# Second products of the first two expert tiles in front of the first products of tiles 2 and 3, in a fused two-layer Flamingo block

## The chip, the cores and the metric

The kernel runs on one NeuronCore of one Trainium2 chip. The metric is the device time of one execution in microseconds. Each kernel is run several times and the median counts; beside it stands one execution taken by the hardware profiler, from which all profile lines come.

## The reference

Inputs are x (4 x 512 x 512, float32) and the weights of four sublayers, each added to x behind a gate. The first three (an int8-quantised product pair, a ternary feed-forward, and cross attention with 16 heads) are not touched here. The last is a mixture of 8 experts, of which each token takes two:

```python
router_in = norm_w * (xf * rsqrt(mean(xf * xf) + EPS))
probs = softmax(router_in @ router_w.T)
topw, topi = top_k(probs, 2);  topw = topw / sum(topw)
cw = zeros((T, E)).at[arange(T)[:, None], topi].add(topw)
g = einsum('td,edf->tef', flat, gate_w);  u = einsum('td,edf->tef', flat, up_w)
expert_out = einsum('tef,efd->ted', silu(g) * u, down_w)
y = einsum('ted,te->td', expert_out, cw) * 4
x = x + tanh(g_ffn[1]) * y
```

T is 2048 tokens, D is 512, and the hidden width of an expert is 256.

## The kernel before

The four batches (512 tokens each) are worked through layer by layer. Everything up to the attention of the last batch is the same before and after. What matters begins near 1300 us of the profile.

**Routing and sorting.** `route(b)` computes the router of one batch: it first stores the batch's `x` after attention to `out` (L771), normalises the rows (`xnl` for the last batch, L184), turns them with PE (L790) into `xTl` (copies by ACT L126 and DVE L128), multiplies with the router's weights (L807), turns the logits (L819) and ranks the experts. Normalised rows and gate weights go to a table in DRAM, `xtab`. `sort` groups the (token, expert) pairs by expert into tiles of 128 rows. Part "a" sorts the first three batches into 16 full tiles (0 to 15) before the last batch's attention is through; part "b" sorts the rest, when the last batch has been routed. In all 36 tiles are sure to be worked.

**One tile.** `gather` (L1076) fetches the 128 rows of the tile out of `xtab` by an indirect DMA that GpSimd (POOL) issues. `weigh_rows` (L1085, L1086, DVE) finds each row's gate weight in them. The rows are turned, by PE for some tiles (`by_tensor`: 0 to 7, 16 to 19 and the last; `prepare`, L1188 with an ACT copy) and by DVE and 16 DMAs on SP's queue for the others (`turn_rows`, L577 and L1179, four tiles at a time). `expert_in` reads the expert's number into a register of PE (L1090), does the first product (L1093, four matmuls of two passes each), Silu on ACT (L1094) and the product of gate and up with the row weight on DVE (L1095), which gives `hid`. `turn_hidden` turns `hid` with PE (L1188) and DVE copies it (L1189). `expert_out` does the second product (L1215), ACT copies it to `y` (L1219), and POOL issues an indirect DMA that adds `y` to the rows of `out` (L1220). Each such addition is made to wait for the one before it, and the first also for the stores of batches 0 to 2.

**Tiles 0 and 1.** Their first products stand between the last heads of the attention (`start_tile`, L1107 and L1093); `hid0` and `hid1` lie in their own buffers.

**The main loop.** For `j` from 0 on: gathers that are due (four tiles ahead for a tile turned by PE, ten ahead for the others), turns by DVE that are due, `hide` (first product of tile j; at j = 0 those of tiles 0 to 3, of which 0 and 1 are done already), `prepare` of tile j + 1, `turn_hidden` of tile j - 1, `expert_out` of tile j - 2, and two steps of the generators `beside`, which are the routing of the last batch and then the sort of part "b". So tile 0's second product comes at j = 2, tile 1's at j = 3.

**The order on the engines.** A scheduler orders the instructions of all engines from the program by its own priorities; each engine then works its queue in that order, and waits on semaphores where a buffer or a value is not ready. The program's order decides who is the earlier and who the later writer of `out`.

Of the kernel before, what the change touches and what calls it, by code (L numbers as in the profile page):

```python
# [57 lines left out]
def kernel(  # L58
# [82 lines left out]
    def acc_tile():  # L141
        sums_in[0] += 1
        return bank(4 + sums_in[0] % 4)
# [875 lines left out]
    def step_beside():  # L1019
        if beside:  # L1020
            try:
                next(beside[0])
            except StopIteration:
                beside.pop(0)
# [63 lines left out]
    def expert_in(j, xgT, h):  # L1088

        e = nc.tensor.value_load(found[j][1], min_val=0, max_val=NE - 1)  # L1090
        ps = work_tile() if j < len(first_hid) else acc_tile()
        for k in range(KD):
            nc.tensor.matmul(ps, lhsT=xgT[k], rhs=gu[:, bass.ds(e, 1), k, :], start=(k == 0), stop=(k == KD - 1))  # L1093
        nc.scalar.activation(h, ps[:, :FE], AF.Silu)  # L1094
        nc.vector.scalar_tensor_tensor(h, h, row_weight[:, j : j + 1], ps[:, FE:], ALU.mult, ALU.mult)  # L1095
        return e, h
# [3 lines left out]
    hidden, first = {}, {}  # L1100
# [57 lines left out]
    def fetch(j):  # L1158
        got[j] = gather(j, mo.tile([P, ROW], F32, tag="xg", name="xg", bufs=8))

    def turn_rows(j):


        if j in by_tensor:
            return
        g, t = divmod(j, NT)
        if t == 0:
            blocks_of[g] = mo.tile([P, NQ, KD * P], F32, tag="blocks", name="blocks", bufs=2)
        xg, owned = got.pop(j)
        tc.keep_in_program_order(  # L1170
            turn_tile_apart(xg[:, :D], blocks_of[g].rearrange("p c (s t r) -> p c s t r", s=KD, t=NT), t)
        )
        weigh_rows(j, xg, owned)
        if t == NT - 1:
            blocks = blocks_of.pop(g)
            dst = mo.tile([P, NQ * KD * P], F32, tag="turned", name="turned", bufs=2)
            for c in range(NQ):
                for a in range(NQ):
                    nc.sync.dma_start(  # L1179
                        dst[c * Q : (c + 1) * Q, a * KD * P : (a + 1) * KD * P], blocks[a * Q : (a + 1) * Q, c]  # L1180
                    )
            for u in range(NT):
                turned_in[g * NT + u] = [dst[:, k * NT + u :: KD * NT] for k in range(KD)]

    def turn_by_tensor(src, n, dst, copy=nc.vector.tensor_copy):
        tp = work_tile()
        for k in range(n):
            nc.tensor.transpose(tp[:, k * P : (k + 1) * P], src[:, k * P : (k + 1) * P], ident)  # L1188
        copy(dst, tp[:, : n * P])  # L1189
        return [dst[:, k * P : (k + 1) * P] for k in range(n)]  # L1190

    def prepare(j):
        if j in by_tensor and j not in hidden and j not in turned_in:
            dst = mo.tile([P, KD * P], F32, tag="xgT", name="xgT", bufs=2)
            turned_in[j] = turn_by_tensor(got[j][0], KD, dst, nc.scalar.copy)
            weigh_rows(j, *got.pop(j))

    def hide(j):
        if j not in hidden:
            prepare(j)  # L1200
            h = mo.tile([P, FE], F32, tag="hid", name="hid", bufs=3)
            hidden[j] = expert_in(j, turned_in.pop(j), h)

    def turn_hidden(j):
        e, h = hidden.pop(j)
        hT = turn_by_tensor(h, NF, mo.tile([P, NF * P], F32, tag="hidT", name="hidT", bufs=3))
        waiting[j] = (e, hT)
# [3 lines left out]
    def expert_out(j):  # L1211
        e, hT = waiting.pop(j)
        ps = acc_tile()
        for f in range(NF):
            nc.tensor.matmul(  # L1215
                ps, lhsT=hT[f], rhs=dn[:, bass.ds(e, 1), f, :], start=(f == 0), stop=(f == NF - 1)
            )
        y = mo.tile([P, D], F32, tag="y", name="y", bufs=3)
        nc.scalar.copy(y, ps)  # L1219
        add = nc.gpsimd.indirect_dma_start(  # L1220
            yacc,
            bass.IndirectOffsetOnAxis(ap=found[j][0], axis=0),
            y,
            None,
            bounds_check=TOK - 1,
            oob_is_err=False,
            compute_op=ALU.add,
        )
        if j in (0, NA):
            written.extend(stores[-1:] if j else stores[: B - 1])  # L1230
        for w in written:
            tc.add_manual_dep(
                add.ins,
                w.ins.name,
                mybir.DependencyInfo(mybir.DependencyClass.Sync, mybir.DependencyReason.DATA),
                reason="adds to what is there",
            )
        written[:] = [add]
# [10 lines left out]
    for j in range(NSURE + 1):  # L1249
        known = NSEG if len(found) == NSEG else NA  # L1250
        for t in [t for t in to_fetch if t - lead[t] <= j and t < known]:
            fetch(t)
            to_fetch.remove(t)
        while to_turn and to_turn[0] - TURN <= j and to_turn[0] in got:
            turn_rows(to_turn.pop(0))


        if j < NSURE - 1:
            for i in range(NT) if j == 0 else (j,):
                hide(i)  # L1260
        if j and j + 1 < NSURE:
            prepare(j + 1)
        if j:
            turn_hidden(j - 1)
        for i in (j - 2,) if j < NSURE - 1 else (j - 2, j - 1) if j == NSURE - 1 else (j - 1,):
            if i >= 0:
                expert_out(i)
        if j == NSURE - 1:
            hide(j)
        step_beside()  # L1270
        step_beside()
        if j == NA - 4:
            while beside:
                step_beside()

    n = nc.values_load(in_all[0:1, :], min_val=1, max_val=NSEG)  # L1276
    with tc.If(n > NSURE):
        for j in range(NSURE, NSEG):
            fetch(j)
        for j in range(NSURE, NSEG):  # L1280
            hide(j)
            turn_hidden(j)
            expert_out(j)
# [35 lines left out]
```

## Time and profile before

| | us |
|---|---|
| median of 3 runs | 1570.09 (1568.76 to 1570.95) |
| the profiled execution | 1567.48 |
| its span (first to last instruction) | 1565.7 |
| tile 0's first product (L1093) | from 1310.43 |
| first product of tiles 2 and 3 | from 1341.85 |
| router's product of the last batch (L807) | from 1355.88 |
| first addition to `out` (L1220) | 1356.77 |
| first product of tile 4 | from 1362.27 |
| last addition | 1557.47 |

The times in the rows are microseconds from the span's start. In a timeline row stand the start, the length, the engine (PE matmul, PEld weight load, DVE, ACT, POOL, SP; a "q" is its queue), the line, the operation, what it writes and reads, the count, and in brackets how long the engine had been idle and what ended that. In a row of stages stand the stage, its length, the busy time of PE, PEld, DVE, ACT and POOL with their counts, the clock granted to PE, the DMA engines' share and GB/s.

### The profile page before, as it was taken

Reading aid. Unit: us, or ns where it says so; the run is one execution under the profiler, and the core shown is the slowest. Engines: PE = TensorE matmul, PEld = TensorE weight load, DVE = VectorE, ACT = ScalarE, POOL = GpSimd, SP = SyncE. Lnnn points to the kernel's source line nnn. Section 1 sums busy time; section 2 is a strip of 40 time slices with the busy share of each in tenths; the row PEclk is TensorE's granted clock in tenths of the full one; section 3 lists DMA queues with packets and bytes.
Section 4 is the critical chain, followed back from the end, with each engine's and each line's share of the span. In section 5 each row is a group of like instructions: output and inputs, shape, how many; then the busy total and the mean of one; then the engine's idle time right before and its main releaser. Section 6 shows DMA issues by size and latency. Waiting matters only on the chain. (4 is left out here: it accounts for less than half of the span.)

```text
span 1565.7 us, 15898 instructions
## 1 busy us (share of the span) xinstructions
PE 1475.8 (94%) x4294; PEld 740.9 (47%) x4294; DVE 905.0 (58%) x2339; ACT 554.0 (35%) x1141; POOL 414.0 (26%) x540
## 2 busy tenths in 40 slices
PE   4988998899999999999999999999999998899995
PEld 2454656666544444444444444444444443455553
DVE  5898737556275555586565675665668553653320
ACT  3554453444243333253323353333433331412111
POOL 2232314352311113131131141141141111335422
PEclk9999999999999999999999999999999999999998
DMA  8633111013355445475455485475584653567542
GB/s 300 222 116 129 47 41 62 28 41 97 126 160 150 133 138 157 136 218 153 127 151 141 129 223 149 117 187 143 153 233 127 159 146 99 149 115 144 122 89 38
DMA packets 110840, 211.10 MB, mean 135 GB/s; under 512 B 28816, under 2 KB 32912, under 8 KB 110752
## 3 DMA queue, kind: packets, MB, share of 16 engines
q0 software_dynamic: 32736, 97.73, 24.0%
q1 hardware_dynamic: 70224, 100.74, 22.9%
q10 hardware_dynamic: 7792, 11.60, 2.1%
q8 instruction: 37, 0.61, 0.2%
q14 instruction: 51, 0.42, 0.1%
HBM read 95.34 MB, written 34.93 MB: 83 GB/s over the span
## 5 line engine op out<-in xcount | busy, mean ns | idle before, releaser
L674 DVE CUSTOM_DVE_ANT_0 e<-bank,mask_b 128x512 f32<-128x512 f32 x256 | 175.0, 688 | 245.7 <-PE bank L669 245.6
L694 PE MATMUL bank<-eT,v 128*128 128x512 f32 x512 | 230.5, 592 | 2.2 <-DVE nmax L674 2.2
L669 PE MATMUL bank<-kT,qT 128*128 128x512 f32 x512 | 231.1, 593 | 0.0
L708 PE MATMUL bank<-wo,oT 128*128 128x512 f32 x512 | 230.7, 592 | 0.3 <-ACT oT L698 0.3
L677 ACT ACTIVATE e<-e,nmax 128x512 f32<-128x512 f32 x256 | 184.3, 720 | 81.6 <-DVE nmax L674 74.5
L571 DVE STREAM_TRANSPOSE blocks<-e 128x512 f32<-128x512 f32 x256 | 158.9, 677 | 30.7 <-DMA eT<-blocks 26.1
L656 PE MATMUL bank<-gu,wq 128*128 128x512 f32 x384 | 174.9, 594 | 1.2 <-DVE nmax L674 1.2
L694 PEld LDWEIGHTS bank<-eT,v 128*128 128x128 f32 x512 | 97.1, 190 | 125.4 <-issue 109.3
L669 PEld LDWEIGHTS bank<-kT,qT 128*128 128x128 f32 x512 | 97.0, 190 | 123.1 <-issue 114.8
L708 PEld LDWEIGHTS bank<-wo,oT 128*128 128x128 f32 x512 | 97.1, 190 | 122.7 <-issue 120.1
L698 ACT COPY oT<-bank 128x512 f32<-128x512 f32 x64 | 37.4, 584 | 315.9 <-PE bank L694 298.4
L656 PEld LDWEIGHTS bank<-gu,wq 128*128 128x128 f32 x384 | 72.3, 190 | 91.9 <-issue 82.3
L635 POOL DMA_DIRECT2D wq<-in_L_xattn_Wq_dram x64 | 48.5, 758 | 245.8 <-PE bank L656 223.7
L685 DVE TENSOR_SCALAR e<-e,rt 128x512 f32<-128x512 f32 x256 | 108.2, 485 | 2.1
L650 POOL DMA_DIRECT2D wo<-in_L_xattn_Wo_dram x64 | 36.5, 571 | 266.9 <-PE bank L708 260.7
L660 ACT ACTIVATE qT<-bank 128x512 f32<-128x512 f32 x64 | 38.2, 597 | 171.6 <-PE bank L656 165.7
L449 PE MATMUL bank<-pjT,hT 128*128 128x512 f32 x320 | 86.4, 405 | 5.4 <-DVE hT L474 5.4
L462 PE MATMUL bank<-xfT,fcT 128*128 128x512 f32 x320 | 89.8, 410 | 0.0
L1093 PE MATMUL bank<-gu,turned 128*128 x192 | 86.5, 593 | 0.0
L501 PE MATMUL bank<-dn,gu 128*128 128x512 f32 x128 | 68.9, 655 | 10.5 <-ACT dn L503 5.0
L473 POOL TENSOR_TENSOR r<-r 128x512 f32<-128x512 f32 x40 | 41.7, 1044 | 107.8 <-ACT hT L472 83.5
L1093 PEld LDWEIGHTS bank<-gu,turned 128*128 128x128 f32 x192 | 56.4, 295 | 28.0 <-issue 5.7
(361 smaller groups left out, 1896.8 us busy)
## 6 DMA issues: line engine op xcount, KB each, us to landing
eT<-blocks SPq DMA_DIRECT2D x1016, 64.0 KB, 2.6
wq<-in_L_xattn_Wq_dram POOLq DMA_DIRECT2D x64, 256.0 KB, 3.8
wo<-in_L_xattn_Wo_dram POOLq DMA_DIRECT2D x64, 256.0 KB, 3.0
kd<-dn SPq DMA_DIRECT2D x32, 256.0 KB, 2.0
vd<-dn SPq DMA_DIRECT2D x32, 256.0 KB, 2.0
kT<-kd POOLq DMA_DIRECT2D x32, 256.0 KB, 3.6
v<-vd POOLq DMA_DIRECT2D x32, 256.0 KB, 4.1
turned<-blocks SPq DMA_DIRECT2D x96, 64.0 KB, 3.5
```

What stands on the lines that cost most here:

```text
L449: nc.tensor.matmul(outs[t], lhsT=h[:, t * P : (t + 1) * P], rhs=pjT[:, j, :], start=(j == 0 and u == 0), stop=(j == NH - 1 and u == 1),)
L462: nc.tensor.matmul(ps, lhsT=fcT[:, i, j * P : (j + 1) * P], rhs=xT[u][:, i, :], start=(u == 0 and i == 0), stop=(u == 1 and i == KD - 1),)
L501: nc.tensor.matmul(ps, lhsT=lhs(i), rhs=rhs(i), start=(i == 0), stop=(i == KC - 1))
L571: nc.vector.transpose(blocks[:, :, :, t, :].rearrange("p c s r -> p s c r"), src.rearrange("p (s c i) -> p s c i", c=NQ, i=Q))
L656: nc.tensor.matmul(ps, lhsT=th[:, i, :], rhs=xT[:, :, i, :], start=(i == 0), stop=(i == KD - 1))
L669: nc.tensor.matmul(ps, lhsT=qT[:, t * P : (t + 1) * P], rhs=kT, start=True, stop=True)
L674: nc.vector.tensor_tensor_reduce(e, ps, mask_b[b], -1.0, 3.0e38, ALU.add, ALU.min, nmax[:, t : t + 1])
L677: nc.scalar.activation(e, e, AF.Exp, bias=nmax[:, t : t + 1], scale=-1.0, accum_out=total[:, t : t + 1])
L685: nc.vector.tensor_scalar(es[:, t, :], es[:, t, :], rt[:, t : t + 1], None, ALU.mult)
L694: nc.tensor.matmul(ps, lhsT=v[:, s, :], rhs=eT[:, :, s, :], start=(s == 0), stop=(s == NT - 1))
L708: nc.tensor.matmul(sums[b][t], lhsT=oT[:, t * P : (t + 1) * P], rhs=to, start=(n == 0), stop=(n == NHEAD - 1))
L1093: nc.tensor.matmul(ps, lhsT=xgT[k], rhs=gu[:, bass.ds(e, 1), k, :], start=(k == 0), stop=(k == KD - 1))
```

## The change

At j = 0, in front of everything but the gathers and turns that are due, both `turn_hidden` and then both `expert_out` of tiles 0 and 1 are called. The loop then skips these two where their turn came before. `hide` is kept from making them again, since they are no longer in `hidden`. Nothing is computed that was not computed before, and nothing is left out.

```diff
     def hide(j):
-        if j not in hidden:
+        if j not in hidden and j not in first:
             prepare(j)
...
+        if j == 0:
+            for i in first:
+                turn_hidden(i)
+            for i in first:
+                expert_out(i)
         if j < NSURE - 1:
             for i in range(NT) if j == 0 else (j,):
                 hide(i)
         if j and j + 1 < NSURE:
             prepare(j + 1)
-        if j:
+        if j > len(first):
             turn_hidden(j - 1)
         for i in (j - 2,) if j < NSURE - 1 else (j - 2, j - 1) if j == NSURE - 1 else (j - 1,):
-            if i >= 0:
+            if i >= len(first):
                 expert_out(i)
```

## The prediction

> **What bounds the kernel now.** I read the page first, then the busy time by stages of the last 230 us, then the timeline around the first additions, then the single tiles (`out_dram`, `xg`) and line 1090. The page and the stages:
>
> ```profile
> span 1565.7 us, 15898 instructions
> PE 1475.8 (94%) x4294; PEld 740.9 (47%) x4294; DVE 905.0 (58%) x2339; ACT 554.0 (35%) x1141; POOL 414.0 (26%) x540
> ```
>
> ```profile
> 1337.00:1344.00 7.00, 3.79 (x13) 2.02 (x12) 4.12 (x15) 3.84 (x5) 5.17 (x7) 0.81 0.87 273
> 1344.00:1352.00 8.00, 7.94 (x28) 4.03 (x27) 5.14 (x26) 2.44 (x6) 1.88 (x2) 0.95 0.65 230
> 1352.00:1362.00 10.00, 8.98 (x29) 3.29 (x30) 5.86 (x15) 5.19 (x12) 3.59 (x3) 1.00 0.50 122
> 1362.00:1380.00 18.00, 17.30 (x59) 8.58 (x60) 14.60 (x77) 7.25 (x12) 6.81 (x5) 1.00 0.61 125
> 1380.00:1440.00 60.00, 60.00 (x192) 34.84 (x191) 23.07 (x61) 11.54 (x24) 27.94 (x22) 1.00 0.64 129
> 1440.00:1500.00 60.00, 57.03 (x153) 32.20 (x152) 20.97 (x54) 11.24 (x23) 25.33 (x20) 1.00 0.61 122
> ```
>
> PE busy time is the first figure behind the length. PE is the bound: from 1362 to 1440 it has 0.7 us free, so whatever makes tile 4 late stays late. There are free PE microseconds in 1337 to 1344 only (3.2), and these are what the change can fill.
>
> ```profile
> 1338.68 0.39 ACTq L771 DMA_DIRECT2D out_dram<-xlast  x1
> 1341.85 3.42 PE L1093 MATMUL bank<-gu,xgT 128*128 x4 [2.68 <-ACT ln_y L151]
> 1345.24 0.94 POOL L1076 DMA_INDIRECT xg<-xtab,aids  x1 [0.30 <-issue]
> 1345.45 0.17 DVE L1085 TENSOR_TENSOR junk<-xg,aowned 128x8 f32<-128x8 f32 x1 [2.79 <-DMA xg<-xtab,aids]
> 1346.82 0.24 DVE L1085 TENSOR_TENSOR junk<-xg,aowned 128x8 f32<-128x8 f32 x2 [1.01 <-DMA xg<-xtab,aids]
> 1355.88 3.59 PE L807 MATMUL bank<-xTl,rwT 128*8 128x512 f32 x8
> 1356.77 1.63 POOL L1220 DMA_INDIRECT out_dram<-y,aids  x1 [10.58 <-ACT y L1219]
> 1362.27 3.70 PE L1093 MATMUL bank<-gu,xgT 128*128 x8
> ```
>
> The reader should see five things. Tiles 2 and 3 start at 1341.85, after 2.68 us of idle PE, at half pace (3.42 us for 4 passes; the 8 at 1362.27 take 3.70). POOL has issued ten gathers (up to tile 12's) by 1346.2, then waits 10.58 us for the first y. DVE stands still when the row weights (L1085) of a gathered tile come before its rows do, and all DVE work behind them stands too. The router's product (L807) is at 1355.88, and tile 4's first product, behind it on PE, at 1362.27.
>
> ```profile
> 1508.51 1.55 POOL L1220 DMA_INDIRECT out_dram<-y,bids  x1 [4.68 <-DMA out_dram<-y,bids]
> 1514.04 1.55 POOL L1220 DMA_INDIRECT out_dram<-y,bids  x1 [3.98 <-DMA out_dram<-y,bids]
> DMA to landing us min/median/max: 3.1/4.8/5.5
> ```
>
> ```profile
> L1090 PEldq TENSOR_LOAD <-aowner_i x7: 294/300/307, 1331.3 to 1335.6; - x7
> ```
>
> Additions go one at a time: each waits for the one before to land (4.8 us, the last line of the first fence, for `out_dram`), so two in a row start about 5.5 apart. The last line: seven loads of an expert's number on PE's queue, one per (1335.6 - 1331.3)/6 = 0.7 us. They cost nothing there because PE had products queued.
>
> **The change part by part.** The order in which the changed program's instructions stand tells more than the diff. (a) PE: the turns of hid0 and hid1 and the four L1215 products stand in front of the turns of tiles 2 and 3. (b) POOL: after six gathers (2, 3, 4, 8, 9, 10) come additions 0 and 1, and only then the gathers of tiles 5, 11, 6, 12, 7, 13, 14. (c) ACT: the store of `xlast` (L771) now waits for both additions, as a later writer of `out`, and stands in front of tile 3's Silu and the copies of `xTl`. (d) DVE: the row weights of tiles 11, 5, 12 and 6 still stand in front of the first copy of `xTl`. (e) PE: the turn of tile 4's rows waits for that copy, and six L1090 loads stand between it and L807.
>
> Replay from 1337.4, when the last L708 ends in both; starts and lengths not given a source are the timeline's rows of before. PE's queue takes four loads from 1336.0 (hid1 is ready at 1335.9): 4 x 0.7, to 1338.8. DVE turns out hidT 0 and 1 after L712 (ends 1338.65), 0.42 each: 1339.1 and 1339.5. Products: 8 passes of 0.43 from 1339.2 to 1342.7. Turns of tiles 2 and 3: 1.0, to 1343.75. ACT: ln_y to 1341.8, y0 0.6 to 1342.4, y1 to 1343.5, xgT of tile 2 to 1344.1. Their first products: 16 passes, 1344.2 to 1351.1, against 1350.2 before. **So far PE has 4.3 us of later work done for 0.9 us**: this is the gain, and the four cold passes (1.7 us) are part of it.
>
> POOL: addition 0 at 1342.7, lands 4.8 later at 1347.5; addition 1 at 1348.2 (0.75 from landing to start: 5.5 less 4.8), lands at 1353.0. Gathers 0.3 behind its 1.6 us, 1.25 apart (rows 1341.49, 1342.74, 1343.99, 1345.24 before): tile 5 at 1350.1, 11 at 1351.4, 6 at 1352.6, 12 at 1353.9. **Tile 12's was issued at 1345.24 before, so 8.7 us later.** ACT's store of xlast goes at 1353.1, in front of it. Landing of a gather:
>
> ```profile
> DMA to landing us min/median/max: 3.2/4.6/6.6
> ```
>
> The 6.6 is that of gathers behind the same 1 MB store at 1338.68, so it is the nearest row: tile 12 lands at 1360.4, at 4.6 at 1358.5. DVE, which did xnl by 1346 (1350.2 before, held by the two waits shown) and has been idle since 1348 but for what tiles 11 and 5 let through, does two row weights (0.5) and the copy of xTl (0.7): 1361.7. Who waits behind it: PE's turn of tile 4 (1361.8), then six loads with nothing queued on PE, 6 x 0.7 = 4.2, to 1366.0. ACT's wait for the additions (1348.4 to 1353.1, then Silu, two copies, two squares: 1356.7) is hidden under DVE's; if DVE's went, L807 would still not start before 1356.7.
>
> L807 then starts on a PE idle for over 8 us but for 4 turns; as at 1341.85 four passes go at 0.85: 8 passes take 5.1 in place of 3.6, to 1371.1. Row copy, turn (L819) and tile 5's rows: 1362.27 less (1355.88 + 3.6) is 2.8 before, with 1.9 of second products in it that are gone now, and about 1.9 for the chain through ACT after: tile 4's products at 1373.0, **10.7 late**. With the gather at 4.6 it is 8.8. Back: tile 5's turn (0.4) is done, and the 0.7 us that PE waited in 1362 to 1380 (for the router's chain) is covered: 1.1. Sum 7.7 to 9.6; I take 9.
>
> After that nothing gives way: 60.00 of 60 busy. Additions follow y and are 5.5 apart at the least, as before; that two are done early buys nothing, because addition 2 needs tile 2's second product, which is behind tile 4's first. The bank, y and hidT buffers change numbers only; SP's turned blocks (from 1370 before, used at 1386) move with DVE's and have the same lead: no cost, and if that were gone each us would add to the loss.
>
> A rule speaks for less. The Trainium skill, "DMA: Bandwidth & Descriptors", section "Anatomy of one DMA — SWDGE (gpsimd) path", puts a transfer from GpSimd at about 2.0 us and its bytes at 436 GB/s: an estimate of 2.6 us for these 256 KB. The rows show 4.8, 4.6 and 6.6. By the rule addition 1 would start at 1346.0, tile 12 be gathered at 1351.7 and land at 1354.3, 6 us earlier, and the loss be about 3 us. I go by the rows.
>
> Against its own time: profiled run 1567.48, span 1565.7 (1.8 outside). Span after 1574.7, run 1576.5. The median shown, 1570.09, is 2.6 above that run; so 1579.
>
> **The rivals.** *Gathers land fast* (chance 0.17): additions at 3.1, gathers at 3.2, the least of both lines. Then tile 12 lands at 1355.4, xTl at 1356.6, loads to 1361, L807 to 1366, tile 4 at 1368: +5.7 - 1.1 = +4.6, 1574.7. For it: gathers at 1335.24 had an idle queue. Against: the xlast store falls among them. *It is given back* (0.07): on top of that, PE's free 3.0 us in 1440 to 1500 is regained; 1.6 left, no measurable change, 1571.7. Against: that idle is a circle of addition, gather, row weights, hid and product, which shifts as a whole. *Faster* (0.05): DVE's row weights do not hold the copy of xTl, because tile 12's rows are there by 1351. Then L807 could follow the turns of xnl at 1353.2, tile 4 start at about 1358.5, and with the 1.1 the gain is near 5: 1565. It decides at 1351, and needs ACT's store not to hold its copies either. Against: POOL cannot issue that gather before addition 0 has landed. That the additions do not come first at all is excluded by POOL's order. The main case has 0.71.
>
> **How the numbers follow.** Likeliest 1579. The main case, with the gather at 4.6 or 6.6, and cold passes or not (1.5), and some us more from loads that take 1.28 as one did before, spans +6 to +13: 1576 to 1583. The range reaches down to the fast gathers with a part given back: 1573 to 1583.5; left out are no change, faster, and a longer pause. Under 0.2% (3.1 us) is what this kernel's timing cannot tell from none. Slower 0.87 (main, fast gathers less a little), same 0.08, faster 0.05.
>
> **What would show it.** Right: addition 0 near 1343 and addition 1 some 5.5 later; tile 12's gather behind both, near 1354; xlast's store near 1353; DVE idle for some 10 us in 1348 to 1361 on gathers; PE idle for some 12 us between 1353 and 1366, then L807 slow; tile 4's L1093 at 1371 to 1373; PE full from there and the last addition about 9 later. Wrong: L807 before 1358, the second addition under 4 us behind the first, or a PE that makes the delay good before 1440.

## The result, and the profile after

The changed kernel takes 1574.61 us in the median of 13 runs (1571.84 to 1581.51), the kernel before 1567.37 us in 13 runs beside them (1563.13 to 1570.95). The ratio is 1.0052, with a 95% interval of 1.0039 to 1.0066: 7.2 us slower by the medians, 6 to 10 us by the interval. The profiled execution took 1572.03 us with a span of 1570.2 us.

In this execution everything up to the change runs 2.6 us ahead of the profile before: the last group of L708, which nothing in the change touches, starts at 1332.19 in place of 1334.80. All comparisons of places below are made from the start of that group; "late" means later than before, counted so.

The stages after. The columns are the stage, its length, busy time and count of PE, PEld, DVE, ACT and POOL, PE's granted clock, the DMA engines' share, GB/s:

```profile
1337.00:1344.00 7.00, 6.71 (x23) 3.31 (x22) 6.23 (x27) 3.23 (x6) 2.90 (x3) 1.00 0.65 149
1344.00:1352.00 8.00, 6.17 (x27) 3.49 (x25) 0.00 (x0) 1.98 (x5) 5.16 (x5) 1.00 0.86 244
1352.00:1362.00 10.00, 1.11 (x4) 0.71 (x4) 3.72 (x13) 3.88 (x10) 3.10 (x4) 0.54 0.56 186
1362.00:1380.00 18.00, 16.60 (x50) 6.57 (x51) 10.95 (x61) 6.01 (x11) 2.61 (x2) 0.88 0.18 40
1380.00:1440.00 60.00, 60.00 (x192) 34.85 (x192) 28.47 (x81) 12.01 (x24) 26.23 (x21) 1.00 0.62 126
```

The free PE time in 1337 to 1344 is filled, as the change wants. Then PE works 1.11 us in the ten from 1352 to 1362, where it worked 8.98 before, at a clock of 0.54, and the clock is 0.88 in the stage after. DVE does nothing at all from 1344 to 1352. From 1380 on PE is full again, as before, so what was lost by then has little room to come back.

The timeline of the changed kernel, POOL, then ACT with its queue, then DVE, then PE (start, length, engine, line, operation, in brackets the idle time before it and what ended that):

```profile
1339.94 1.62 POOL L1220 DMA_INDIRECT out_dram<-y,aids  x1 [1.36 <-issue]
1345.62 1.56 POOL L1220 DMA_INDIRECT out_dram<-y,aids  x1 [4.05 <-ACT hid L1094]
1351.32 0.95 POOL L1076 DMA_INDIRECT xg<-xtab,aids  x1 [0.30 <-issue]
...
1350.38 0.38 ACTq L771 DMA_DIRECT2D out_dram<-xlast  x1
1350.81 0.38 ACT L1094 ACTIVATE hid<-bank 128x256 f32<-128x256 f32 x1 [5.40 <-DMA out_dram<-y,aids]
...
1352.66 0.24 DVE L1085 TENSOR_TENSOR junk<-xg,aowned 128x8 f32<-128x8 f32 x2 [8.67 <-DMA xg<-xtab,aids]
1357.38 0.24 DVE L1085 TENSOR_TENSOR junk<-xg,aowned 128x8 f32<-128x8 f32 x2 [3.91 <-DMA xg<-xtab,aids]
1357.74 0.68 DVE L128 COPY xTl<-bank 128x512 f32<-128x512 f32 x1
...
1341.29 7.13 PE L1093 MATMUL bank<-gu,xgT 128*128 x16 [0.29 <-ACT xgT L1189]
1358.48 1.11 PE L1188 MATMUL bank<-ident,xg 128*128 128x128 f32 x4 [8.31 <-DVE xTl L128]
1362.77 5.37 PE L807 MATMUL bank<-xTl,rwT 128*8 128x512 f32 x8 [3.18 <-issue]
1369.64 3.60 PE L1093 MATMUL bank<-gu,xgT 128*128 x8
```

The chain is read from top to bottom. Addition 1 goes out 5.68 us behind addition 0. The brackets of POOL's second row name ACT, but in the program that addition waits for addition 0 to land, and the 5.68 us fit the 5.5 between two additions in the rows before. The gather of tile 12 is the fourth behind the additions, at 1351.32. Its rows are what DVE waits for at 1357.38, after 8.67 and 3.91 us of standing still. Right behind them on DVE comes the first copy of `xTl`, and PE, idle for 8.31 us, turns tile 4's rows. Then PE has no products to do while it loads six registers (3.18 us, "issue"), and does L807 in 5.37 us where it took 3.59 before. Tile 4's first product starts 37.5 us after the last L708 group, 10.0 us late. ACT waits too: the store of `xlast` goes out at 1350.38, once addition 1 has landed, and the next Silu comes after 5.40 us of idle time. That wait ends 7 us before DVE's, so it could not be the one that counted, unless DVE's were gone.

### The profile page after: what moved, and what is told of

It is laid out like the page before. It is cut to its first block, busy times and chain, and to the rows that moved or that the text cites. A ratio compares the mean times of both kernels' runs of the same rounds, so it can differ in the third digit from the quotient of the medians.

```text
span 1570.2 us, 15884 instructions
## 1 busy us (share of the span) xinstructions
PE 1473.6 (94%) x4285; PEld 739.8 (47%) x4294; DVE 904.8 (58%) x2339; ACT 553.8 (35%) x1141; POOL 413.4 (26%) x540
## 5 line engine op out<-in xcount | busy, mean ns | idle before, releaser
L708 PE MATMUL bank<-wo,oT 128*128 128x512 f32 x512 | 230.7, 592 | 0.1
L571 DVE STREAM_TRANSPOSE blocks<-e 128x512 f32<-128x512 f32 x256 | 158.9, 677 | 28.8 <-DMA eT<-blocks 23.2
L708 PEld LDWEIGHTS bank<-wo,oT 128*128 128x128 f32 x512 | 97.1, 190 | 122.5 <-issue 120.1
```

Of the source, the lines that this page charges most:

```text
L571: nc.vector.transpose(blocks[:, :, :, t, :].rearrange("p c s r -> p s c r"), src.rearrange("p (s c i) -> p s c i", c=NQ, i=Q))
L708: nc.tensor.matmul(sums[b][t], lhsT=oT[:, t * P : (t + 1) * P], rhs=to, start=(n == 0), stop=(n == NHEAD - 1))
```

## The experiments

The theory: the two additions hold POOL, so the gathers of tiles 5, 11, 6 and 12 are late; DVE has their row weights in its queue in front of the `xTl` copies, and so the lateness goes over to the router, PE and tile 4. The rivals: ACT's wait at the store of `xlast`; the products in front and PE's own order; each moved tile simply costing its share. Each ratio is against runs of the kernel before from the same session. There were four sessions, in which the kernel before had medians of 1567.37 (the changed kernel's), 1572.51, 1566.64 and 1572.10 us, so kernels are compared by their ratios.

| kernel | L807 from | tile 4 from | tile 4 late | ratio, 95% interval |
|---|---|---|---|---|
| before | 21.1 | 27.5 | | |
| changed | 30.6 | 37.5 | 10.0 | 1.0052 [1.0039, 1.0066] |
| products alone in front | 21.2 | 26.4 | -1.1 | 0.9979 [0.9966, 0.9992] |
| the same again | 21.4 | 26.6 | -0.8 | 0.9983 [0.9969, 0.9998] |
| changed, store first | 28.5 | 34.8 | 7.3 | 1.0037 [1.0026, 1.0049] |
| changed, weights later | 24.1 | 31.3 | 3.8 | 1.0000 [0.9984, 1.0016] |
| before, one gather twice | 28.2 | 34.6 | 7.1 | 1.0040 [1.0028, 1.0052] |
| changed, tile 0 only | 27.5 | 34.2 | 6.7 | 1.0033 [1.0015, 1.0052] |
| changed, store first and weights later | 23.2 | 28.4 | 1.0 | 1.0014 [1.0003, 1.0026] |
| products alone, weights later | 20.3 | 25.5 | -2.0 | 0.9996 [0.9984, 1.0007] |
| the same, store first | 23.5 | 28.7 | 1.2 | 0.9992 [0.9980, 1.0005] |
| products alone, all late weights later | 20.3 | 25.5 | -2.0 | 0.9980 [0.9969, 0.9992] |

Places are microseconds after the start of the last L708 group, from one profiled execution each (their starts: before 1334.80, changed 1332.19, then down the table 1335.53, 1334.11, 1334.35, 1338.57, 1334.98, 1333.32, 1331.38, 1335.07, 1334.30 and 1337.64). Line numbers of some kernels are a few higher behind the edit.

### The products in front, the additions left where they were

```diff
     def expert_out(j):
...
         nc.scalar.copy(y, ps)
-        add = nc.gpsimd.indirect_dma_start(
+        made[j] = y
+
+    def add_out(j):
+        y = made.pop(j)
+        add = nc.gpsimd.indirect_dma_start(
...
             if i >= len(first):
                 expert_out(i)
+            if i >= 0:
+                add_out(i)
```

> The second products of tiles 0 and 1 and their copies to y come in front as in the changed kernel; the two additions stay where they were before, behind the ten gathers. Theory (the additions ahead of the gathers of tiles 5, 11, 6, 12 on POOL hold the row weights on DVE, and with them the first xTl copy): the loss is gone. The first xTl copy is back at some 15 us after the turn of tile 1's hid rows, the router's product L807 follows at full rate, and with the idle 2.7 us in front of L1093 filled by the products the time is 2 us under the kernel before (1 us over to 4 us under). Rival 'ACT's wait at the store of xlast': the loss is gone too, as the store again comes ahead of the additions. Rival 'the moved products and PE's order themselves': 5 to 7 us slower than before, as in the changed kernel.

Its timeline:

```profile
1345.98 0.95 POOL L1076 DMA_INDIRECT xg<-xtab,aids  x1 [0.30 <-DMA out_dram<-xlast]
1347.24 1.63 POOL L1225 DMA_INDIRECT out_dram<-y,aids  x1 [0.30 <-DMA xg<-xtab,aids]
1354.45 0.68 DVE L128 COPY xTl<-bank 128x512 f32<-128x512 f32 x1
1356.70 3.60 PE L807 MATMUL bank<-xTl,rwT 128*8 128x512 f32 x8 [0.61 <-DVE xTl L128]
1361.90 3.60 PE L1093 MATMUL bank<-gu,xgT 128*128 x8
```

The ten gathers are out by 1345.98, 10.5 us after the last L708 group as before (10.4), and the addition follows them. L807 runs at full rate (3.60) and tile 4 is 1.1 us early. The kernel is faster than before by 0.2%, 3.2 us by the medians (1569.32 against 1572.51), and the second time by 0.17%. So the products in front are the good half of the change, and the rival that blames them falls. This run takes away both DVE's late gathers and ACT's wait at the store; the next ones separate the two. The first copy of `xTl` on DVE comes 16.3 us after the turn of tile 1's hid rows at 1338.11 (15 expected), behind a product that waits for ACT's Silu.

### ACT's wait taken away

```diff
         if j == 0:
+            step_beside()
             for i in first:
                 turn_hidden(i)
...
         step_beside()
-        step_beside()
+        if j:
+            step_beside()
```

> As the changed kernel, but the first step of the last batch's router (the store of xlast, L771, and its layer statistics) is called ahead of the early products, so ACT doesn't wait for additions; addition 0 now waits for that store to land. Theory (POOL and DVE): the additions end some 3 to 4 us later than in the changed kernel, so the gathers of 5, 11, 6, 12 and the first xTl copy are later by as much; six register loads in a row in front of L807 are only one now (3.2 us back): 5 to 9 us slower than the kernel before, no better than the changed one. Rival 'ACT's wait': within 2 us of the kernel before.

```profile
1344.94 1.62 POOL L1220 DMA_INDIRECT out_dram<-y,aids  x1 [4.23 <-ACT y L1219]
1350.62 1.56 POOL L1220 DMA_INDIRECT out_dram<-y,aids  x1 [4.06 <-issue]
...
1338.23 0.39 ACTq L771 DMA_DIRECT2D out_dram<-xlast  x1
1356.15 0.58 ACT L126 COPY xTl<-bank 128x512 f32<-128x512 f32 x1
...
1359.92 0.24 DVE L1085 TENSOR_TENSOR junk<-xg,aowned 128x8 f32<-128x8 f32 x2 [1.49 <-DMA xg<-xtab,aids]
1360.61 0.68 DVE L128 COPY xTl<-bank 128x512 f32<-128x512 f32 x1
...
1340.24 0.30 PE L1188 MATMUL bank<-ident,xg 128*128 128x128 f32 x1 [2.93 <-issue]
1340.44 5.39 PE L1215 MATMUL bank<-dn,hidT 128*128 x8
1361.35 1.11 PE L1188 MATMUL bank<-ident,xg 128*128 128x128 f32 x4 [5.47 <-DVE xTl L128]
```

The store goes out at 1338.23 and ACT's two copies of `xTl` are through by 1357; still the kernel is 0.37% slower, and PE again waits for DVE's copy behind the row weights. ACT's wait alone is not the cause. The expectation had the register loads gone but for one. They did not go away: they now stand in front of the products, with 2.93 us of idle PE and 5.39 us for eight passes that take 3.70 in the changed kernel. That puts the additions 2.8 us later than in the changed kernel, so this run doesn't tell what ACT's wait costs, only that the loss is there without it.

### The row weights taken out of the way

```diff
-                evacuate(xT[:, :, t, :], tp.rearrange("p (k q) -> p k q", k=KD))
+                turned_last.append(evacuate(xT[:, :, t, :], tp.rearrange("p (k q) -> p k q", k=KD)))
...
-        nc.vector.tensor_tensor(junk, xg[:, D:], owned, ALU.mult)
+        w = nc.vector.tensor_tensor(junk, xg[:, D:], owned, ALU.mult)
+        for t in turned_last if j in (5, 6, 11, 12) else ():
+            tc.add_manual_dep(w.ins, t.ins.name, ...)
```

> As the changed kernel, but the row weights of tiles 5, 6, 11 and 12 wait on DVE until the four xTl copies are done; POOL's order and the additions are left as in the changed kernel. Theory (it is the row weights in front of the xTl copy that pass the lateness of the gathers on): the xTl copy on DVE comes when PE has turned the rows, those on ACT at 1351.5 (behind the store of xlast that waits for the additions), L807 at about 1356 to 1357 where the changed kernel has 1362.8; 2 us slower than before (0 to 4). Rivals 'ACT's wait alone' and 'PE's order': 6 to 8 us slower, as in the changed kernel.

```profile
1355.71 0.69 DVE L128 COPY xTl<-bank 128x512 f32<-128x512 f32 x1 [3.41 <-PE bank L790]
1357.14 0.38 ACTq L771 DMA_DIRECT2D out_dram<-xlast  x1
1359.55 0.58 ACT L126 COPY xTl<-bank 128x512 f32<-128x512 f32 x1
1362.71 5.62 PE L807 MATMUL bank<-xTl,rwT 128*8 128x512 f32 x8 [5.59 <-issue]
```

The register loads around L807, first in the changed kernel, then here:

```profile
L1090 PEldq TENSOR_LOAD <-aowner_i x7: 294/301/308, 1358.5 to 1362.8; - x7
L1095 PEldq TENSOR_LOAD <-aowner_i x7: 299/308/1400, 1356.5 to 1362.7; - x7
```

POOL still works in the changed kernel's order, and its gathers are as late. But DVE's copy now waits for PE alone, and no loss against before can be measured: ratio 1.0000, and L807 lies 6.4 us under the changed kernel's place, as expected. The row weights are the link. (The gain of the products alone, some 0.2%, isn't there either.) Two things are left behind DVE's hold. ACT's second copy ends at 1360.13, behind the store that waits for the additions: the second hold was there all along, covered by the first. But L807 starts 2.6 us after that copy. What ends last in front of it are PE's register loads, which begin at 1356.5, before ACT's copies, and run one after another. Three of them take 1.40, 0.92 and 0.56 us in place of 0.30, just after the store went out at 1357.14; in the changed kernel, where none does, the same row of loads ends 4.1 us after its start, here 6.1. At the changed kernel's pace they would have ended near 1360.6 (an estimate), about when ACT's copy does. So the 3.8 us at tile 4 are the loads' and ACT's together; that the store is what slows the loads is read from these rows, and no run shows it apart.

### Late gathers alone

The kernel before, with nothing moved:

```diff
             fetch(t)
             to_fetch.remove(t)
+            for _ in range(1 if t == 5 else 0):
+                gather(5, got[5][0])
```

> The kernel before, with one thing added: the gather of tile 5 is issued twice into the same tile, the second waiting for the first to land, so that POOL holds the gathers of 11, 6 and 12 for some 6 us; nothing of PE, ACT or the additions is moved. Theory: the row weights reach DVE 6 us later, the first xTl copy goes from 1351.3 to about 1357, L807 and tile 4 are as late, and of the 6 us about 4 stay at the end: 4 us slower than before (2.5 to 6). Every rival that blames the moved products, ACT's wait or the additions themselves: within 1 us of the kernel before.

```profile
1347.35 0.94 POOL L1076 DMA_INDIRECT xg<-xtab,aids  x1 [4.75 <-DVE ln_d L156]
1356.85 0.24 DVE L1085 TENSOR_TENSOR junk<-xg,aowned 128x8 f32<-128x8 f32 x2 [3.76 <-DMA xg<-xtab,aids]
1357.95 0.69 PE L1188 MATMUL bank<-ident,hid 128*128 128x128 f32 x2 [5.56 <-DVE xTl L128]
1363.21 3.60 PE L807 MATMUL bank<-xTl,rwT 128*8 128x512 f32 x8
```

The last row weights and the copy behind them in the kernel before:

```profile
1350.48 0.23 DVE L1085 TENSOR_TENSOR junk<-xg,aowned 128x8 f32<-128x8 f32 x2
1351.33 0.69 DVE L128 COPY xTl<-bank 128x512 f32<-128x512 f32 x1
```

One wait on POOL, of 4.75 us, with the program of PE, ACT and the additions as before, costs 0.40%, against 0.52% in the changed kernel. (It also fetches one tile's rows, 256 KB, a second time.) The last row weights come at 1356.85 (1350.48 before), and PE stands still for 5.56 us. The loss is above the range of 2.5 to 6 us (6.8 by the medians, 1579.29 against 1572.51): tile 4 is 7.1 us late, and the expectation's 2 us that come back are not seen.

### One tile in place of two

```diff
         if j == 0:
-            for i in first:
+            for i in [0]:
                 turn_hidden(i)
-            for i in first:
+            for i in [0]:
                 expert_out(i)
...
-        if j > len(first):
+        if j > 1:
             turn_hidden(j - 1)
...
-            if i >= len(first):
+            if i >= 1:
                 expert_out(i)
```

> As the changed kernel, but only tile 0 has its product and addition in front; tile 1's stay at their old place. One addition then stands ahead of the gathers of 5, 11, 6, 12. Theory: what costs is the second addition's wait for the first (5.7 us) ahead of the gathers; with one, the gather of tile 12 goes out some 12 us after the last L708 begins (10.4 before, 19.1 in the changed kernel), the first xTl copy is at most 2 us later than before: 1 us slower than before (1.5 under to 3 over). If instead each moved tile costs its share, half of the changed kernel's loss: 4 us slower.

This missed: 1.0033, some 5 us. The stores on ACT's queue, the fourth gather behind the addition, DVE's waits, and a stage in between:

```profile
1342.89 0.37 ACTq L852 DMA_DIRECT2D xtab<-xnl  x1
1345.30 0.38 ACTq L771 DMA_DIRECT2D out_dram<-xlast  x1
...
1346.55 0.95 POOL L1076 DMA_INDIRECT xg<-xtab,aids  x1 [0.30 <-issue]
1350.73 0.25 DVE L1085 TENSOR_TENSOR junk<-xg,aowned 128x8 f32<-128x8 f32 x2 [7.44 <-DMA xg<-xtab,aids]
1354.37 0.24 DVE L1085 TENSOR_TENSOR junk<-xg,aowned 128x8 f32<-128x8 f32 x2 [3.19 <-DMA xg<-xtab,aids]
...
1347.00:1351.00 4.00, 2.69 (x19) 1.92 (x17) 0.27 (x3) 2.97 (x8) 0.49 (x1) 1.00 1.03 371
```

The gather goes out 13.2 us after L708, about where it was expected (12). But it lands 7.8 us later, where the changed kernel's took 6.1. The two stores of 1 MB, 11.6 us apart before, went out 2.4 us apart here, among the gathers, and the DMA engines are full (1.03 of their time, 371 GB/s). So an addition in front of the gathers costs twice: it holds the gathers back, and it holds the store of `xlast` back into their way. The second part is read from these rows; no run took the store away alone. By its time this run can't refuse the rival, which said 4 us: the interval is 2 to 8. What speaks against a share per tile is the path: DVE stands still for the same gather as with both tiles, PE then waits 7.63 us for the same copy, and tile 4 is late by 6.7 us, not by half of 10.0.

### Both holds off, and the products alone with later weights

The first is the changed kernel with both edits from above, the others are the kernel with the products alone and the edit of the row weights for tiles 4 to 6 and 8 to 12.

> As the changed kernel, additions early on POOL, with the edits of 'store first' and of 'weights later' together: neither ACT nor DVE waits for additions or late gathers in front of the xTl copies. Theory (DVE's row weights, and right behind them ACT's wait at the store, are all that costs): L807 at about 22 us after the last L708 begins, and the time is that of the kernel with the products alone, 3 us under before (5 under to 0). If the early additions or the late gathers cost in another way too (traffic, a tile that comes too late for PE): 2 us slower than before or more.

> The kernel with the products in front and the additions at their old place, with the row weights of tiles 4 to 6 and 8 to 12 behind the four xTl copies on DVE. There the weights and what follows them on DVE still hold the norm of the last batch (xnl, L184) until 1351 and so ACT's table load and the xTl copies: with them behind, xnl comes 2 us earlier, PE runs from L790 into the tile-4 turn and L807 without the 1.4 and 0.6 us of idle time: 2 us under the kernel with the products alone, 5 us under before (7 to 2 under). If something else on ACT holds the copies: the same as with the products alone, 3 us under.

> As the one with the weights behind the copies, with the first step of the last batch's router (store of xlast and layer statistics) called ahead of the early products as well. The layer statistics come earlier on DVE; but the loads of PE's registers then stand in front of the products (2.9 us of idle time in the run with the store first alone). The two about cancel: 4 us under before (7 under to 0).

All three came out slower than the middle of what was expected, by 3 to 5 us, and the first two missed their ranges. The first (1.0014, expected 5 us under before to none) came out on the side of its second forecast, that something else costs too: DVE's and ACT's holds are not all. With both holds off, then with the products alone and later weights (three rows of each):

```profile
1337.64 0.30 PE L1193 MATMUL bank<-ident,xg 128*128 128x128 f32 x1 [3.31 <-issue]
1354.61 3.60 PE L807 MATMUL bank<-xTl,rwT 128*8 128x512 f32 x8
1367.61 1.12 PE L1220 MATMUL bank<-dn,hidT 128*128 x2 [2.91 <-DVE hidT L1194]
```

```profile
1355.35 3.60 PE L807 MATMUL bank<-xTl,rwT 128*8 128x512 f32 x8 [0.99 <-DVE junk L1085]
1363.31 0.17 DVE L1085 TENSOR_TENSOR junk<-xg,aowned 128x8 f32<-128x8 f32 x1 [0.95 <-DMA xg<-xtab,aids]
1368.07 1.25 PE L1221 MATMUL bank<-dn,hidT 128*128 x2 [2.62 <-DVE hidT L1194]
```

In the first, the pause at the router is gone: of the 10.0 us, 9.0 are back at tile 4. What stays is the register loads in front of the products (3.31 us idle, then slow passes as in the run with the store first), and a new wait of 2.91 us. That these two are the rest of the loss is read from the rows; the loads came in front with the edit that moves the store. In the second, tile 4 comes 2.0 us early, and at 1368.07 PE waits 2.62 us for the copy of turned hid rows. The row above tells why: row weights of tiles 7, 13 and 14, whose gathers stand behind the second addition, wait on DVE until 1363.3 in front of the routing, and the copy stands behind that. The third has the loads in front of the products too (3.30 us of idle time), and no long wait behind tile 4; it ends level with before.

### All late row weights moved

```diff
-        nc.vector.tensor_tensor(cw, cw, wide(mx), ALU.mult)
+        routed[:] = [nc.vector.tensor_tensor(cw, cw, wide(mx), ALU.mult)]
...
-        for t in turned_last if j in (4, 5, 6, 8, 9, 10, 11, 12) else ():
+        for t in turned_last if j in (4, 5, 6, 8, 9, 10, 11, 12) else routed if j in (7, 13, 14) else ():
```

> As the kernel with the products in front, the additions at their old place and the row weights of tiles 4 to 6 and 8 to 12 behind the xTl copies; now the row weights of tiles 7, 13 and 14 stand behind the last batch's routing on DVE as well. In the kernel without that they waited for their gathers until 1363.3 in front of the routing's first step (L821), and with it the copy of tile 4's turned hid rows: PE stood still for 2.6 us and then ran at half clock. Theory (a row weight that waits for a late gather holds whatever is behind it on DVE): the routing starts 3 us earlier, that idle time goes, 4 us under before (6 to 1 under). If the idle time comes from the length of the routing chain itself: no gain, within 1.5 us of before.

> The kernel with the products alone in front once more, on the same chip and against the same runs of before as the one with all late row weights moved: 3 us under before, as the first time (5 to 1 under).

```profile
1366.77 0.38 PE L1193 MATMUL bank<-ident,hid 128*128 128x128 f32 x2
1366.98 1.88 PE L1221 MATMUL bank<-dn,hidT 128*128 x4
```

The wait of 2.62 us is gone: the second products follow the turn at once, at full pace. The ratio is 0.9980, against 0.9996 with those weights left in front. So by the trace the same mechanism, a row weight that waits for a late gather and holds the rest of DVE's queue, made that wait. That it cost time is not shown: the two ratios are from different sessions, and their intervals overlap. Against the products alone (0.9983 in the same session) it makes no difference that can be measured; the 1 us that it is ahead at tile 4 is not seen at the end. Both beat the kernel before by some 3 us and the changed one by 0.7%.

## Why the prediction was right

**Direction and main case.** Slower was forecast, by 9 us (1579 against 1570.09); measured is 7.2 us more than before. In absolute time the forecast lies 4.4 us above the 1574.61 measured, and 2.7 us of that are its starting point: the median of the kernel before is 1567.37 over 13 runs, where the first three gave 1570.09. The main case came, through the wait that it named.

**The steps.** Moved back by the 2.6 us of this execution, the forecast had addition 0 at 1340.1 (1339.94), addition 1 at 1345.6 (1345.62), the gather of tile 12 at 1351.3 (1351.32), the end of the `xTl` copy at 1359.1 (1358.4), L807 at 1363.4 (1362.77) with a length of 5.1 (5.37), and tile 4 at 1370.4 (1369.64). In brackets what the profile shows. Landing was taken as 6.6 us from the gathers behind the same store; it was 6.1. So 10.7 us late became 10.0.

**The rule that spoke for less.** By the prediction's estimate from the Trainium skill ("DMA: Bandwidth & Descriptors", section "Anatomy of one DMA — SWDGE (gpsimd) path"), the additions would have been 3.3 us apart and the loss about 3 us. The additions are 5.68 apart here and the interval starts at 6 us. The rows of the trace before were the better price.

**ACT under DVE.** "If DVE's went, L807 would still not start before 1356.7": with the row weights later, ACT's second copy ends at 1360.13, with an execution 3.8 us later at L708, so at 1356.4. The hidden second wait and its size were right. L807 itself came at 1358.9, counted so, because the register loads in front of it ended later still; the forecast had priced loads at 0.7 us each, and three took longer there.

**What was mis-sized.** The lateness was forecast 0.7 us too large, mainly by the landing. The loss of 9 us itself lies inside the measured 6 to 10. The term "Back: 1.1" can't be checked so finely. From tile 4's first product to the span's end it is 203.4 us before (1362.27 to 1565.7) and 200.6 after (1369.64 to 1570.2), which would be some 2.8 back. But the two profiles of the kernel with the products alone take 206.4 and 205.6 us for this stretch, though its medians are below those of the kernel before; what single executions show there is too coarse for a term of 1.1. "After that nothing gives way" holds for 1380 to 1440 (60.00 of 60). How much comes back later, and at which wait, is not settled here.

**The gain.** "4.3 us of later work done for 0.9" was right in kind: with the additions left at their place, the products alone gain about 3 us. The rival "faster" named two conditions, that DVE's row weights don't hold the copy of `xTl` and that ACT's store doesn't; the kernel with the products alone fulfils both, and the changed one neither.

## What to carry to other kernels

Moving a step earlier moves all of it: look at what its last instruction waits for, on which queue, and what stands behind it there. Here the product was worth moving and the addition, which waits for the one before, was not; split the two. Where an in-order engine has small work on late data in front of work that others wait for, every delay of that data is passed on, so such work belongs behind. That paid where the data was late (1.0000 in place of 1.0052); with the gathers on time it gained nothing that could be measured (0.9996 and 0.9980, against 0.9979 and 0.9983). And take a second wait into account that only the first one hides.

## What the runs showed of the hardware that was not expected

- Idle PE time of 2.6 us and more was followed by slow passes (eight in 5.21 to 5.62 us behind 2.93 to 5.59 us of idle time, against 3.60 to 3.70; four in 3.42 behind 2.68); after 0.99 us L807 still took 3.60. The granted clock was 0.54 in the stage around the longest such pause of the changed kernel.
- Register loads cost about 3 us where PE had nothing else to do: 3.18 us in front of L807 in the changed kernel, 2.93 to 3.31 in front of the products with the store first, and 5.59 with the row weights later, where three loads took 0.56 to 1.40 us in place of 0.30. Moving other work only changed the place.
- The gather of tile 12 was waited for until 3.6 us after its issue where the last store of 1 MB had gone out 7.9 us earlier (store first), 6.1 right behind one such store, and 7.8 behind two.
